# Causal attention with a two-layer local stack: side work placed one slot apart, one scratch buffer for the masked maxima, a second buffer for the outputs' second turn

## Chip, cores and metric

The kernel runs on one core of a Trainium2 chip. The metric is the device time of one execution in microseconds (us), the median of three runs.

## What is computed

An input x of 4 batches of 1024 tokens with 256 features goes through two residual blocks. The change touches only the first. Cut to that block:

```python
x = x + attn(layernorm(x))

def attn(x):                                   # B, T, D, H = 4, 1024, 256, 16 heads of 16
    q, k, v = heads(x @ wq + bq), heads(x @ wk + bk), heads(x @ wv + bv)
    scores = einsum('bhqd,bhkd->bhqk', q, k) / sqrt(16)
    p = softmax(scores + causal_mask, axis=-1)
    return merge(einsum('bhqk,bhkd->bhqd', p, v)) @ wo + bo

x = x + ffn_stack(layernorm(x))                # two layers of local attention (window 128) and gated FFN
```

All is float32. The second block starts from a layer norm of the first block's result; the first stage therefore hands over `y_sb`, that norm already taken, and a copy of x in device memory.

## The kernel before

The whole order of work is written out by hand (`tc.manual_schedule`): each engine executes its instructions in the order in which the program issues them. The first stage (the causal stage) ends at about 728 us of the trace, the rest is the local stack.

**Chunks and slots.** The causal stage goes through 16 chunks `n` (4 batches of 4 groups of 4 heads) in `NU` = 12 slots each, after a lead-in chunk `n` = -1. In slot `u` of chunk `n`, `pair(n, u, 0)` and `pair(n, u, 1)` issue on TensorE the transposed scores `t` of chunk `n` (for the exponentials) and the plain scores `s` of chunk `n + 1` (for the row maxima), two heads of each at a time (L417). ScalarE takes the exponential of `t` (L441), GpSimd zeroes what lies above the diagonal (L447, the select), and VectorE takes the maximum of `s`: with a plain reduction where no mask is needed (L435), else with an operation that adds the mask, writes the sum to a scratch tile `junk` that nothing reads, and leaves the maximum in `nmax` (L429). Each of these is followed by a short instruction that reads out the accumulator. Slots 0 to 3 and 8 to 11 have masked maxima of 512, 384, 256 and 128 columns (four each), slots 4 to 7 plain ones. The score tiles `s` have four banks of PSUM, shared with the projections; the tiles `t` have three. `products` (L480) multiplies the exponentials of two slots before (`LAG` = 2) with the values; its sum is copied to `avs` (L491).

**Side work.** At the end of slot `u`, the list `plan[n][u]` is issued. `put(n, u, fn, ...)` fills it; a slot number of 12 and more falls into the next chunk. The pieces are:

- `project`, `prep_b`: queries, keys and values of the next heads or the next batch, on TensorE with a copy on ScalarE; `prep_b` also has one GpSimd addition (L329).
- `norm(b, t0, t1)`: layer norm statistics of two tiles of x on VectorE (L263, L264, L158), then a power on GpSimd (L160). `prep_x`: the normalised tile `xn`, two on GpSimd (L274). `turn_x`: VectorE's 32 by 32 transposes of two tiles (L297), and on the second half of a group 16 DMAs on SP (L307) into `xnT`.
- `put_maxima`: a transpose of `nmax` on VectorE (L458) and five DMAs that put the maxima into the query tile.
- `put_out`: first turn of a finished output, `avs` to `t1`, on VectorE (L497), the reciprocal of the row sums (L499) and GpSimd's multiplication (L500). `put_oT`: second turn, `t1` to `t3`, on VectorE (L509), and four DMAs on SP into `oT` (L512).
- `out_b`: the output projection on TensorE (`pr`), a copy to `add` on ScalarE (L532) and the residual on GpSimd (L533); for the last two tile pairs of the last batch one addition by VectorE instead (L529). `out_s`: statistics on VectorE (L540, L541) and a power on GpSimd. `out_c`: `y_sb`, two GpSimd operations (L556).
- `spread`: DMAs that lay queries and keys out in strips; `scale_tab`: a multiplication of a table for the second block on GpSimd (L117), in chunk 5 only.

Three lists matter for the change: what the first chunk of a batch (c = 0) and the one behind it (c = 1) do for the next batch, the two turns of the outputs in every chunk, and what is left behind the last slot of chunk 15, which the schedule issues by hand. `a1`, `a2` and so on are pools of one, two and more buffers per tag; a tile of a tag takes the next of its buffers, and its first writer waits until the one who used that buffer last is done.

Of the kernel before, what the change touches and what calls it, by code (L numbers as in the profile page):

```python
# [10 lines left out]
F32 = mybir.dt.float32  # L11
# [5 lines left out]
P = 128  # L17
B, T, D = 4, 1024, 256
# [31 lines left out]
def kernel_body(  # L50
# [122 lines left out]
    with actx:  # L173
# [62 lines left out]
        NCH = B * NC4  # L236
# [96 lines left out]
        def bias():  # L333

            pb = one("pbias")
            for c in range(2):
                nc.tensor.transpose(
                    pb[:, c * P : (c + 1) * P], rows_c[:, 0, c * P : (c + 1) * P], ident
                )
            bv = a2.tile([P, 512], F32, tag="junk", name="bv")  # L340
            nc.scalar.copy(bv[:, 0:D], pb[:, 0:D])
            po = one("pbias_o")
            for c in range(2):
                nc.tensor.matmul(
                    po[:, 0:D], lhsT=bv[:, c * P : (c + 1) * P], rhs=wo_sb[:, c, :],
                    start=(c == 0), stop=(c == 1),
                )
            nc.vector.tensor_tensor(rows_c[:, 1, :], po[:, 0:D], rows_c[:, 1, :], ALU.add)
# [32 lines left out]
        def pair(n, u, pr):  # L381

            first, final = n < 0, n + 1 == NCH
            if (first or final) and pr:
                return
            th = () if first else range(4) if final else (2 * pr, 2 * pr + 1)
            sh = () if final else range(4) if first else (2 - 2 * pr, 3 - 2 * pr)  # L390

            def bank(pool, h):
                p, tag = ((pat, "t"), (pas, "s"))[pool]
                return p.tile([P, 512], F32, tag=tag, name=f"{'ts'[pool]}_{n}_{u}_{h}")

            todo = []
            if th:
                qb, kt = UNITS_T[u]
                c0 = max(0, kt * P - qb * 512)
                ts = {h: bank(final and h % 2, h) for h in th}  # L400
                for j, h in enumerate(th):
                    r = slice(32 * h, 32 * h + 32)
                    todo.append((j, 0, ts[h][:, c0:512], kTs(n)[r, kt * P : (kt + 1) * P],
                                 qTs(n)[r, qb * 512 + c0 : (qb + 1) * 512]))
            if sh:
                i, piece = UNITS_M[u]
                k0 = piece * 512
                k1 = min(k0 + 512, (i + 1) * P)
                w = k1 - k0
                diag = k1 == (i + 1) * P and piece == i // 4  # L410
                ss = {h: bank(not (first and h % 2), h) for h in sh}
                for j, h in enumerate(sh):
                    r = slice(32 * h, 32 * h + HD)
                    todo.append((j, 1, ss[h][:, 0:w], qTs(n + 1)[r, i * P : (i + 1) * P],
                                 kTs(n + 1)[r, k0:k1]))
            for j, _, o, lhsT, rhs in sorted(todo, key=lambda x: x[:2]):
                nc.tensor.matmul(o, lhsT=lhsT, rhs=rhs, start=True, stop=True)  # L417
            if sh:
                if i >= 4 and piece == 0 and pr == 0:
                    mxs[n + 1, i] = a5.tile([P, 4], F32, tag="mx", name=f"mx_{n + 1}_{i}")  # L420
                for h in sh:
                    first_of_two = i >= 4 and piece == 0
                    if first_of_two:
                        acc = mxs[n + 1, i][:, h : h + 1]
                    else:
                        acc = nmax[:, piece, 4 * h + i % 4 : 4 * h + i % 4 + 1]
                    if diag:
                        junk = a2.tile([P, 512], F32, tag="junk", name=f"junk_{n}_{u}_{h}")
                        nc.vector.tensor_tensor_reduce(  # L429
                            out=junk[:, 0:w], in0=ss[h][:, 0:w], in1=mask_c[:, 512 - w : 512],  # L430
                            scale=1.0, scalar=mxs[n + 1, i][:, h : h + 1] if piece else -3.0e38,
                            op0=ALU.add, op1=ALU.max, accum_out=acc,
                        )
                    else:
                        nc.vector.tensor_reduce(acc, ss[h][:, 0:w], AX.X, ALU.max)  # L435
                if piece and (pr or first):
                    del mxs[n + 1, i]
            for h in th:
                if h % 2 == 0:
                    et = a8.tile([P, 2, 512], F32, tag="et", name=f"et_{n}_{u}_{h}")  # L440
                nc.scalar.activation(et[:, h % 2, c0:512], ts[h][:, c0:512], AF.Exp, scale=ASCALE)  # L441
                if h % 2 == 0:
                    continue
                if kt >= 4 * qb:

                    d = et[:, :, c0 : c0 + P]
                    nc.gpsimd.affine_select(  # L447
                        out=d, in_=d, compare_op=ALU.is_ge, fill=0.0, base=0,
                        pattern=[[0, 2], [1, P]], channel_multiplier=-1,
                    )  # L450
                if h == 1:
                    avs_[n, u] = ([], c0)
                avs_[n, u][0].append(et)
# [51 lines left out]
        def put_oT(n, qb):  # L505

            b, c = divmod(n, NC4)
            t3 = a1.tile([P, 512], F32, tag="t3", name=f"t3_{n}_{qb}")
            nc.vector.transpose(t3, avs_.pop((n, "t1", qb)).rearrange("p q s -> p (q s)"))  # L509
            for j in range(4):  # L510
                r = (c % 2) * 64 + j * HD
                nc.sync.dma_start(  # L512
                    oT[r : r + HD, c // 2, qb * 512 : (qb + 1) * 512],
                    t3[STRIP * j : STRIP * j + HD, :],
                )

        def out_b(b, t2):

            pr = one(f"pr_{b}_{t2}")
            t0 = 2 * t2  # L520
            for i in range(2):
                for c in range(2):
                    strips(
                        pr[:, i * D : (i + 1) * D], oT[:, c, (t0 + i) * P : (t0 + i + 1) * P],
                        wo_sb[:, c, :], c,
                    )
            xt = xs[b][:, t0 : t0 + 2, :]
            if b == B - 1 and t2 >= 2:
                nc.vector.tensor_tensor(xt, pr.rearrange("p (i d) -> p i d", i=2), xt, ALU.add)  # L529
                return  # L530
            add = a1.tile([P, 2, D], F32, tag="add", name=f"add_{b}_{t2}")
            nc.scalar.copy(add, pr.rearrange("p (i d) -> p i d", i=2))  # L532
            nc.gpsimd.tensor_tensor(xt, xt, add, ALU.add)  # L533
# [31 lines left out]
        def put(n, u, fn, *a):  # L565

            plan[n + u // NU][u % NU].append((fn, a))

        def outs(n, u, b, t2):
            put(n, u, out_b, b, t2)  # L570
            put(n, u + 1, out_s, b, t2)
            put(n, u + 3, out_c, b, t2)

        def quarters(n, b, d, first, *slots):
            for i, u in enumerate(slots):
# [2 lines left out]
        for n in range(NCH):  # L578
            b, c = divmod(n, NC4)
            more = b + 1 < B  # L580
            if n >= 1:
                put(n, 2, put_out, n - 1, 1)
                put(n, 3, put_oT, n - 1, 1)
            if n + 1 < NCH:
                put(n, 4, put_maxima, n + 1, 0)
                put(n, 11, put_maxima, n + 1, 1)
            put(n, 6, put_out, n, 0)
            put(n, 7, put_oT, n, 0)
            if c == 0:
                if b:  # L590
                    quarters(n, b, 1, 3, 0, 2, 4, 6, 8)
                    outs(n, 7, b - 1, 2)
                    outs(n, NU, b - 1, 3)
                    put(n, 1, spread, n + 2, 0)
                    put(n, 3, spread, n + 3, 0)
# [4 lines left out]
                put(n, 9, spread, n + 2, 1)  # L600
                put(n, NU, spread, n + 3, 1)
            if c == 0 and more:
                for i, u in enumerate((5, 7, 9, 10)):
                    put(n, u, norm, b + 1, 2 * i, 2 * i + 2)
                put(n, 8, prep_x, b + 1, 0)
                put(n, 10, turn_x, b + 1, 0, 0)
                put(n, 10, prep_x, b + 1, 1)
                n += 1
                put(n, 0, turn_x, b + 1, 0, 1)
                put(n, 1, prep_x, b + 1, 2)  # L610
                put(n, 2, prep_x, b + 1, 3)
                put(n, 3, turn_x, b + 1, 1, 0)
                put(n, 4, turn_x, b + 1, 1, 1)
                quarters(n, b + 1, 0, 0, 5, 6, 8, 10)
                n += 1
                quarters(n, b + 1, 0, 4, 0, 2, 3, 4)
# [6 lines left out]
                quarters(n, b + 1, 1, 0, 3, 5, 7)  # L623
                n -= 3
            if c == 3:
                outs(n, 9, b, 0)
                outs(n, 11, b, 1)
        n = -1
        plan[n][0] = [(project, (0, 0, i, 3)) for i in range(2)]
        plan[n][0] += [(spread, (0, 1, nc.scalar)), (spread, (1, 0)), (spread, (1, 1))]  # L630
# [19 lines left out]
        with tc.manual_schedule(  # L650
# [42 lines left out]
            for w in range(LAG, 0, -1):  # L693
                products(NCH - 1, NU - w)
            left = [x for u in plan[NCH] for x in u]
            for fn, a in left[0:1]:
                fn(*a)
            put_out(NCH - 1, 1)
            for fn, a in left[1:]:
                fn(*a)  # L700
            put_oT(NCH - 1, 1)
            for fn in (out_b, out_s, out_c):
                for t2 in (2, 3):
                    fn(B - 1, t2)
# [646 lines left out]
```

## Time and profile before

| what | value |
|---|---|
| median of 3 runs | 1962.36 us (1960.04 to 1964.89) |
| the profiled execution, its own time | 1962.94 us |
| its span in the trace | 1960.9 us |
| granted TensorE clock over the span | 0.97 |
| TensorE, matmul busy | 1888.3 us (96%) |
| VectorE busy | 1350.1 us (69%) |
| ScalarE busy | 1005.1 us (51%) |
| GpSimd busy | 1031.2 us (53%) |
| causal stage, lead-in and preparation included | to about 728 us |
| last output's DMA of the causal stage | 724.7 to about 728.6 us |

How to read it: all times of the trace are microseconds from the span's start. PE is TensorE's matmuls, PEld its weight loads, DVE is VectorE, ACT is ScalarE, POOL is GpSimd, SP is SyncE, which here issues nearly all DMAs. L429 is line 429 of the kernel. A timeline's line has start, duration, engine, line, operation, output and inputs, shape and count, and in brackets the idle time of the engine before it with what ended it. In a table of windows each line has the busy time and the number of instructions of each engine, and after them the clock that TensorE was granted (1.00 is full speed, 0.50 half). Matmuls of this stage use a quarter of TensorE's rows or columns, and in the trace up to four of them overlap, so that the busy share stays near full even when only one of the four runs.

### The profile page before, as it was taken

How to read it: one execution, taken by the hardware profiler on the slowest of the kernel's cores; microseconds unless marked ns; L12 is line 12 of the kernel's file. 1: busy time of each engine (PE TensorE's matmuls, PEld its weight loads, DVE VectorE, ACT ScalarE, POOL GpSimd, SP SyncE). 2: the span in 40 equal slices, each digit the busy share in tenths (PEclk: the TensorE clock that was granted, in tenths of full speed). 3: DMA queues.
4: the chain of work that ended last, by engine and by line, in shares of the span. 5: the costliest groups of instructions: out<-in, count | busy, mean ns of one | idle time of the engine just before them, and what ended most of it. 6: DMA issues, size and time to landing. Idle time of an engine off the chain costs nothing.

```text
span 1960.9 us, 51320 instructions
## 1 busy us (share of the span) xinstructions
PE 1888.3 (96%) x19234; PEld 1031.0 (53%) x19234; DVE 1350.1 (69%) x4092; ACT 1005.1 (51%) x2646; POOL 1031.2 (53%) x1268
## 2 busy tenths in 40 slices
PE   8999999999999978899899999999999999999999
PEld 5333333333333335556566665666566566566575
DVE  6766776677677825666776787687677677677633
ACT  1546545564565654454455545545554554554521
POOL 3322362245234138675775676676675676676621
PEclk8979989998999988999999999999999999999999
DMA  4122111212201001155555555555565655665520
GB/s 119 22 34 75 26 33 32 61 24 36 62 12 28 10 32 67 27 93 90 93 97 99 88 103 99 117 106 103 102 143 100 105 110 104 116 109 95 101 49 22
DMA packets 797927, 144.43 MB, mean 74 GB/s; under 512 B 766336, under 2 KB 788592, under 8 KB 797168
## 3 DMA queue, kind: packets, MB, share of 16 engines
q1 hardware_dynamic: 797424, 140.89, 37.1%
q8 instruction: 153, 2.51, 0.5%
q14 instruction: 94, 0.77, 0.1%
q10 hardware_dynamic: 256, 0.26, 0.1%
HBM read 21.25 MB, written 8.65 MB: 15 GB/s over the span
## 4 chain that ended last, share of the span: by engine, by line
PE 86%; SPq 4%; DVE 3%; issue 2%; POOL 2%; ACT 1%; DMA 1%; DVEq 0%; POOLq 0%; ACTq 0%
PE t L417 15%; PE pag L1151 15%; PE pf L1175 8%; PE av L480 7%; PE pw L1061 6%; PE pq L792 5%; PE pk L792 5%; PE pv L792 5%; PE plo L1019 4%; PE ls L939 4%; SPq L891 3%; PE pp L251 3%; PE pv L251 2%; PE s L417 2%; PE pr L251 2%
## 5 line engine op out<-in xcount | busy, mean ns | idle before, releaser
L441 ACT ACTIVATE et<-t 128x512 f32<-128x512 f32 (+2 forms) x744 | 327.7, 490 | 232.5 <-PE s L417 210.9
L417 PE MATMUL t<-qbuf,kbuf 32*128 32x512 f32 (+2 forms) x1488 | 396.3, 552 | 2.5 <-ACT et L441 2.4
L417 PE MATMUL s<-kbuf,qbuf 16*128 16x512 f32 (+3 forms) x1440 | 382.1, 554 | 1.5 <-DVE mx L435 1.1
L1151 PE MATMUL pag<-hnT,w 128*128 128x512 f32 x704 | 312.5, 593 | 0.8 <-DVE hnT L1135 0.8
L972 ACT ACTIVATE e<-e,lnmx 128x192 f32<-128x192 f32 (+2 forms) x512 | 224.1, 439 | 48.7 <-DVE lnmx L965 48.2
L417 PEld LDWEIGHTS t<-qbuf,kbuf 32*128 32x128 f32 x1488 | 143.9, 189 | 168.9 <-ACT et L441 111.5
L447 POOL TENSOR_SCALAR_AFFINE_SELECT et<-et 128x256 f32<-128x256 f32 x256 | 103.0, 410 | 221.4 <-ACT et L441 221.1
L986 POOL TENSOR_SCALAR e<-e,lrsum 128x192 f32<-128x192 f32 (+2 forms) x512 | 206.7, 430 | 20.1 <-DVE lrsum L983 14.7
L1151 PEld LDWEIGHTS pag<-hnT,w 128*128 128x128 f32 x704 | 131.9, 191 | 143.1 <-issue 134.9
L480 PE MATMUL av<-et,v_sb 128*32 128x256 f32 (+5 forms) x2240 | 186.8, 405 | 6.5 <-POOL et L447 4.7
L435 DVE TENSOR_REDUCE mx<-s 128x1 f32<-128x512 f32 x240 | 153.1, 681 | 57.2 <-PE s L417 55.0
L831 POOL TENSOR_TENSOR rn<-ss,mhalf 128x16 f32<-128x16 f32 x64 | 188.1, 2940 | 5.3
L1175 PE MATMUL pf<-w,act 128*128 128x256 f32 x768 | 173.1, 379 | 0.0
L828 POOL TENSOR_TENSOR rot<-rot,m 128x1024 f32<-128x1024 f32 x64 | 151.3, 2365 | 35.4 <-DVE m L809 29.7
L1175 PEld LDWEIGHTS pf<-w,act 128*128 128x128 f32 x768 | 145.8, 190 | 26.6 <-issue 7.2
L1165 DVE SCALAR_TENSOR_TENSOR act<-pag,cols_sb,ge 128x512 f32<-128x512 f32 x80 | 59.3, 741 | 142.3 <-ACT ge L1164 98.7
L429 DVE CUSTOM_DVE_ANT_0 junk<-s,mask_c 128x512 f32<-128x512 f32 (+3 forms) x240 | 106.7, 484 | 62.4 <-PE s L417 59.6
L417 PEld LDWEIGHTS s<-kbuf,qbuf 16*128 16x128 f32 x1440 | 141.8, 189 | 10.8 <-DVE mx L435 4.6
L429 DVE CUSTOM_DVE_ANT_0 junk<-s,mask_c,mx 128x512 f32<-128x512 f32 (+3 forms) x240 | 120.9, 546 | 37.6 <-PE s L417 36.4
L965 DVE CUSTOM_DVE_ANT_0 e<-ls,mask_h 128x192 f32<-128x192 f32 x408 | 116.9, 350 | 23.6 <-PE ls L939 23.6
L480 PEld LDWEIGHTS av<-et,v_sb 128*32 128x32 f32 x2240 | 45.4, 109 | 164.1 <-issue 116.0
L1061 PE MATMUL pw<-wlo,loT 128*128 128x256 f32 x512 | 128.6, 394 | 0.8 <-ACT loT L1052 0.7
(294 smaller groups left out, 3372.4 us busy)
## 6 DMA issues: line engine op xcount, KB each, us to landing
ring_sb<-turned SPq DMA_DIRECT2D x896, 96.0 KB
qbuf<-dense SPq DMA_DIRECT2D x128, 32.0 KB
oT<-t SPq DMA_DIRECT2D x128, 32.0 KB
x_keep<-x SPq DMA_DIRECT2D x4, 1024.0 KB
xr<-x_keep SPq DMA_DIRECT2D x8, 512.0 KB
out_dram<-y_sb SPq DMA_DIRECT2D x16, 256.0 KB
kbuf<-dense SPq DMA_DIRECT2D x120, 32.0 KB
x<-in_x_dram SPq DMA_DIRECT2D x3, 1024.0 KB
```

The source lines that it names most:

```text
L417: nc.tensor.matmul(o, lhsT=lhsT, rhs=rhs, start=True, stop=True)
L429: nc.vector.tensor_tensor_reduce(out=junk[:, 0:w], in0=ss[h][:, 0:w], in1=mask_c[:, 512 - w : 512], scale=1.0, scalar=mxs[n + 1, i][:, h : ...
L435: nc.vector.tensor_reduce(acc, ss[h][:, 0:w], AX.X, ALU.max)
L441: nc.scalar.activation(et[:, h % 2, c0:512], ts[h][:, c0:512], AF.Exp, scale=ASCALE)
L480: nc.tensor.matmul(av[32 * j : 32 * j + 32, lo:hi], lhsT=v_sb[b % 2][:, kt, VW * (4 * c + j) : VW * (4 * c + j) + STRIP], rhs=ets[j // 2][ ...
L792: nc.tensor.matmul(pq[i], lhsT=lhs[c], rhs=wt[:, c, i * INNER : (i + 1) * INNER], start=(c == 0), stop=(c == 1),)
L831: nc.gpsimd.tensor_tensor(rn[:, :, 0], ss, mhalf, ALU.pow)
L972: nc.scalar.activation(e[:, i, lo:nk], e[:, i, lo:nk], AF.Exp, bias=nmx[:, h : h + 1], scale=-1.0, accum_out=sums[:, h : h + 1],)
L986: nc.gpsimd.tensor_scalar(e[:, i, lo:nk], e[:, i, lo:nk], rsum[:, h : h + 1], 1.0, ALU.mult, ALU.mult)
L1061: nc.tensor.matmul(pw[:, 0:D], lhsT=oT[:, c, :], rhs=wt[:, c, :], start=(c == 0), stop=(c == 3))
L1151: nc.tensor.matmul(pg[half], lhsT=wt[:, c, ff * P : (ff + 1) * P], rhs=hnT[:, c, :], start=(c == 0), stop=(c == 1),)
L1175: nc.tensor.matmul(pf[:, 0:D], lhsT=act[:, f, i * P : (i + 1) * P], rhs=wt[:, f, :], start=(f == 0), stop=(f == NF - 1),)
```

## The change

- The scratch tile `junk` has one buffer instead of two. The tile `bv` of `bias` moves to the tag `add`.
- `put_oT` comes two slots after `put_out` instead of one (slots 4 and 8 instead of 3 and 7), and its tile `t3` has two buffers instead of one.
- In chunks with c = 0, the four `norm`s move from slots 5, 7, 9, 10 to 0, 1, 3, 5; the four `prep_x` from 8, 10, 13, 14 to 7, 9, 12, 14; the four halves of `turn_x` from 10, 12, 15, 16 to 10, 11, 15, 17.
- `out_b`, `out_s`, `out_c` of the first tile pair move from slots 9, 10, 12 to 10, 11, 13 of the last chunk of a batch; for the second and third pair `out_s` and `out_c` come one slot later.
- All residuals of the last batch are added by VectorE.
- Behind the last slot, `put_out` and `put_oT` of the last output come ahead of the rest.

```diff
-            bv = a2.tile([P, 512], F32, tag="junk", name="bv")
+            bv = a1.tile([P, 512], F32, tag="add", name="bv")
...
-                        junk = a2.tile([P, 512], F32, tag="junk", name=f"junk_{n}_{u}_{h}")
+                        junk = a1.tile([P, 512], F32, tag="junk", name=f"junk_{n}_{u}_{h}")
...
-            t3 = a1.tile([P, 512], F32, tag="t3", name=f"t3_{n}_{qb}")
+            t3 = a2.tile([P, 512], F32, tag="t3", name=f"t3_{n}_{qb}")
...
-            if b == B - 1 and t2 >= 2:
+            if b == B - 1:
...
-        def outs(n, u, b, t2):
+        def outs(n, u, b, t2, wait=1):
             put(n, u, out_b, b, t2)
-            put(n, u + 1, out_s, b, t2)
-            put(n, u + 3, out_c, b, t2)
+            put(n, u + wait, out_s, b, t2)
+            put(n, u + wait + 2, out_c, b, t2)
...
-                put(n, 3, put_oT, n - 1, 1)
+                put(n, 4, put_oT, n - 1, 1)
...
-            put(n, 7, put_oT, n, 0)
+            put(n, 8, put_oT, n, 0)
...
-                    outs(n, 7, b - 1, 2)
+                    outs(n, 7, b - 1, 2, 2)
...
-                for i, u in enumerate((5, 7, 9, 10)):
+                for i, u in enumerate((0, 1, 3, 5)):
                     put(n, u, norm, b + 1, 2 * i, 2 * i + 2)
-                put(n, 8, prep_x, b + 1, 0)
+                put(n, 7, prep_x, b + 1, 0)
+                put(n, 9, prep_x, b + 1, 1)
                 put(n, 10, turn_x, b + 1, 0, 0)
-                put(n, 10, prep_x, b + 1, 1)
+                put(n, 11, turn_x, b + 1, 0, 1)
                 n += 1
-                put(n, 0, turn_x, b + 1, 0, 1)
-                put(n, 1, prep_x, b + 1, 2)
+                put(n, 0, prep_x, b + 1, 2)
                 put(n, 2, prep_x, b + 1, 3)
                 put(n, 3, turn_x, b + 1, 1, 0)
-                put(n, 4, turn_x, b + 1, 1, 1)
+                put(n, 5, turn_x, b + 1, 1, 1)
...
-                outs(n, 9, b, 0)
-                outs(n, 11, b, 1)
+                outs(n, 10, b, 0)
+                outs(n, 11, b, 1, 2)
...
-            for fn, a in left[0:1]:
+            put_out(NCH - 1, 1)
+            put_oT(NCH - 1, 1)
+            for fn, a in left:
                 fn(*a)
-            put_out(NCH - 1, 1)
-            for fn, a in left[1:]:
-                fn(*a)
-            put_oT(NCH - 1, 1)
```

## Prediction

> Terms: chunk c0 to c15 is one round of twelve slots in the causal stage (batch times four plus head group), s0 to s11 its slots; the lead-in before c0 has scores only.
>
> **What bounds the kernel now.** I read the page first, then the busy time and granted clock of one window per chunk, then windows of 3.4 us around the places where the clock fell, then the timelines there. Busy shares say little: PE is at 96% everywhere. The table by chunk says more (columns: window, length, busy us and count of PE, PEld, DVE, ACT, POOL, then PE's clock, DMA share, GB/s).
>
> ```profile
> 92.60:142.40 49.80, 49.58 (x416) 17.35 (x412) 32.57 (x105) 23.75 (x55) 15.83 (x26) 0.73 0.20 33
> 268.40:320.30 51.90, 48.66 (x436) 17.00 (x432) 33.34 (x110) 24.50 (x56) 26.24 (x34) 0.84 0.19 32
> 446.40:494.90 48.50, 47.14 (x438) 16.88 (x434) 33.24 (x110) 24.52 (x56) 21.69 (x32) 0.86 0.20 35
> 619.70:656.70 37.00, 36.45 (x399) 14.24 (x395) 29.85 (x96) 22.48 (x52) 13.62 (x25) 1.00 0.08 17
> 656.70:692.10 35.40, 34.85 (x376) 13.51 (x372) 28.73 (x91) 21.86 (x51) 7.67 (x18) 1.00 0.12 40
> ```
>
> c1, c5 and c9 take 49.8, 51.9 and 48.5 us, c13 (same place in its batch, no next batch to prepare) 37.0. Four projections of about 1 us each (two take 1.93 in the chain of waits) explain 4.2; so c5 loses 10.7, c9 7.3, and c1, which has no 1.9 us output projection, 10.5. Their clock is 0.73 to 0.86. The windows around c5's start show how:
>
> ```profile
> 263.40:266.80 3.40, 3.36 (x39) 1.58 (x37) 3.29 (x14) 1.70 (x7) 3.40 (x6) 1.00 0.10 23
> 266.80:270.20 3.40, 3.28 (x33) 1.60 (x34) 3.30 (x18) 1.29 (x4) 3.40 (x5) 1.00 0.00 0
> 270.20:273.60 3.40, 3.40 (x18) 0.72 (x17) 1.72 (x7) 0.61 (x2) 3.40 (x5) 0.50 0.02 2
> ```
>
> DVE (3.3 of 3.4) and POOL (3.4) are full for 6.8 us, PE starves for score banks, and the clock is halved from 270.2 to 277.0. The same happens at 96.1 (27.3 us long, until c1's first projections) and at 447.7 (6.8 us). Two more falls, at 290.6 and 468.1, follow a wait for POOL. The timelines show the two kinds of wait:
>
> ```profile
> 93.83 0.18 PEld L417 LDWEIGHTS s<-kbuf,qbuf 16*128 16x128 f32 x1 [0.95 <-DVE nmax L429]
> ...
> 463.33 0.77 DVE L297 STREAM_TRANSPOSE xturn<-xn 128x256 f32<-128x256 f32 x2
> 466.96 0.71 DVE L509 STREAM_TRANSPOSE t<-t 128x512 f32<-128x512 f32 x1 [2.86 <-POOL t L500]
> ```
>
> So the stage is PE-bound, with VectorE's lateness deciding where the clock falls.
>
> **The change, part by part.** Durations are this profile's; its span is 1960.9 and its own time 1962.9, 2.0 around it and 0.6 above the median.
>
> *Second turn of outputs two slots on.* At 466.96 DVE stood 2.86 us behind L500 on POOL. In c9 the multiply would be done some 9.9 us into s1, and DVE reaches the turn in s4 at about 10.6: the wait goes, and with it the fall at 468.1 (c9's s5 lasts 8.7 us, c13's 3.2, a projection 1.0: 4.5 too long). In c5 the fall at 290.6 has another cause, POOL's table scaling (2.36 us twice); it stays, and the queue is now add 1.28, two xn 2.45, scale 2.36 in s0, so the selects of s1 and s2 come some 2.7 us late instead of 2.16: gain 0, from -1 to +2.
>
> *Spread of norm, prep_x, turn_x.* A norm costs DVE 1.45 (264.24 to 265.69), an out_s 1.27, a turn_x 0.68, the two turns of outputs 0.9 and 0.6. Before, s9, s10 of c4 held norm, norm and turn_x. After, s9 to s11 hold out_s, turn_x, turn_x; for c0 only the two turns. Second halves of turn_x issue 16 DMAs on SP at 0.6 us each (four take 2.4) one slot sooner; ahead of them is the maxima's copy, behind them only copies used a chunk later: 0. But s1 of c4 and c8 now holds out_s and norm together: 2.72 us of DVE.
>
> *One scratch buffer for the masked maxima.* This is the new wait. Masked maxima follow one another without a pause today:
>
> ```profile
> 648.97 0.75 DVE L429 CUSTOM_DVE_ANT_0 junk<-s,mask_c,mx 128x512 f32<-128x512 f32 x1 [0.28 <-PE s L417]
> 649.65 0.08 DVE L429 DVE_READ_ACCUMULATOR2_ANT nmax<- 128x1 f32 x1
> 649.65 0.75 DVE L429 CUSTOM_DVE_ANT_0 junk<-s,mask_c,mx 128x512 f32<-128x512 f32 x1
> ```
>
> Start to start is 0.68, less than one lasts. The view of L429 has this beside its 512 maxima:
>
> ```profile
> L429 DVEq EVENT_SEMAPHORE  x386: 21/21/50, 22.8 to 691.8; - x193
> ```
>
> These are the sequencer's waits for the scratch buffer; in the trace one ends 0.03 us after the accumulator read of the maximum before last, when nothing is lost. With one buffer it must be the last one. What such a wait costs when it binds is seen once:
>
> ```profile
> 736.60 0.42 DVE L540 BATCH_NORM_STATS2 sto<-x 128x6 f32<-128x256 f32 x1
> 737.12 0.18 DVE L541 BATCH_NORM_AGGREGATE mvo<-sto 128x2 f32<-128x6 f32 x1
> ```
>
> 0.10 from end to start behind a sequencer wait. So start to start becomes 0.75 + 0.10 = 0.85: +0.18 (bounds: 0, if PE always keeps DVE waiting, and 0.19). The Trainium skill speaks against this: VectorE: DVE Perf Modes, The DRAIN you can't avoid, measured eight copies with a semaphore after each at the same time as with one after the last, so the semaphore would be free. By that rule this edit costs 0; by the rows, where neighbours overlap by 0.07, 0.18 each. I take the rows. 480 such maxima in c0 to c14 are 86 us of DVE, nearly all beside PE work: a clean slot's DVE work rises from 2.4 to 3.0 us in s0 (slot 3.28), 1.9 to 2.6 in s1 (2.64), 1.1 to 1.8 in s11 (1.79). In c14 DVE still fits into 35.4 (about 33): loss 0.3 at s11. Nothing is left for side work in s1, s2, s10, s11.
>
> *Where it comes through.* Rule used: DVE's lag at the next slot is its lag now, plus its work, minus the slot's length; PE stalls by lag plus first pair of maxima minus slot length. (It gives 0.9 and 1.5 for c4's s10 and s11 before; seen: 0.9 and about 1.3.) After, in c4 and c8: s0 4.4 of work against 3.87, s1 5.2 against 2.64, s2 2.8 against 3.61: the lag reaches 4.3, and PE stalls 0.36, 1.3 and 0.8. At s10, s11: 0.7 and 0.8. In c0, s10 and s11: 0.4.
>
> *Price of a stall.* The Trainium skill, TensorE: Matmul & The Clock Gate, What's actually happening, wants about one idle window (3.4 us) before the clock halves; by it these stalls cost themselves only. The rows show halving after windows with some 1.3 us of starving, and none after stalls of 0.3 to 0.9. I take the rows: 3.4 us more (6.8 at half clock) for a window that loses over 1.1 us.
>
> *Residual by VectorE, last batch.* Two more batches of ACT 0.59 and POOL 1.27 go, two DVE adds of 0.69 come in c15, where DVE is idle: about -1 on ACT, which sets c15. *Tail order.* The multiply waited for the y_sb pair:
>
> ```profile
> 720.90 2.44 POOL L556 TENSOR_SCALAR y_sb<-x,mvo,rs_o 128x256 f32<-128x256 f32 x2
> 723.30 0.62 POOL L500 TENSOR_TENSOR t<-t,rec 128x256 f32<-128x256 f32 x1
> ```
>
> rec ends at 721.4, so -1.9. y_sb's pairs now end near 726.7, before the last projections' adds: hidden. Second t3 buffer and bv's place: 0.
>
> **Sum.** Gains: c1's fall -9.5; c5's and c9's start, where stalls of 1.5 remain and the fall is even odds, -1.9 each; c9's second fall -4.5; tail -3: 20.8. Losses: lead-in, where DVE runs 22.1 to 29.2 and 45.4 to 53.5 without a pause, 30 waits of 0.18 less what PE hides: 4, with a stall and half a fall in c0, 2.5; c4 and c8 2.4 stall and four fifths of a fall each: 10.4; out_s in c5, c9, c13 0.8 each, last chunks 1: 3.4. Together 20.3. Net -0.5 against 1962.9: about 1962.4.
>
> **Rivals.** (1) *The scratch wait does not bind* (PE's banks release the maxima anyway, or the rule holds). Then c4's s1 leaves a stall of 0.4 to 0.7 only, no fall; c1 -10, c5 and c9 -5 each, c9 -4.5, tail -3, second fall of c5 stays: -27, 1936; half of the wait gives some 1950. For it: 139 of the maxima wait for PE's scores (96 us). Against it: at the loaded slots DVE is full. 26%. (2) *Slower: the clock, once halved in c4 and c8, stays down* as at 96.1, where 27.3 us cost 10.5 because no projection came. Two such instead of 2.7 each: +15.6, 1978. It decides once s1 to s3 lose over 1.1 us in one window. Against it: c4 and c8 have projections in s2, s4 and s6, and the falls with projections near lasted 6.8 and 10.2 us. Half of it, with all 30 waits of the lead-in bare (5.4 instead of 4), gives 1971. 36%, other ways to be slower included. (3) *The spreading does not do what it says*: c5's POOL queue, above, at most +2, inside the others. Likeliest, 38%: gains given back, 1962.
>
> **Numbers.** Within 0.3% is 5.9 us, what a measurement can tell. Faster 0.26, same 0.38, slower 0.36. Likeliest case alone: 1956 to 1968. The range takes in half of each rival: 1946 to 1979.
>
> **What would show it.** Masked maxima 0.85 apart instead of 0.68 where DVE is behind, 0.80 without the mx operand. c1 near 40 us at clock 1.00. c4 and c8 longer than 40.9 and 40.6, clock under 1.00 near their s3. The 2.86 us wait at L509 gone. Oddly placed falls, or maxima still 0.68 apart, would prove the sum wrong.

## The result and the profile after

The changed kernel takes 1972.7 us (median of 18 runs, 1964 to 1982 but for one of 2007) against 1962.4 us for the kernel before, run beside it on the same chip: a ratio of 1.005, with a 95% interval of 1.0037 to 1.0064. So it is slower by half a per cent, where 1962 and no difference were forecast. The profiled execution took 1976.7 us with a span of 1975.0; before it was 1962.9 and 1960.9. The span grew by 14.0 us, and all of it can be found chunk by chunk. This execution is 4.0 us above its kernel's median, the one of before 0.6 above: so some 3 of the 14 us may belong to the execution and not to the change.

The table of windows of the changed kernel has the same columns as the one of before (window, length, busy us and count of PE, PEld, DVE, ACT, POOL, PE's clock, DMA share, GB/s). The lines are the lead-in, c1, c4, c5, c8, c9 and c14.

```profile
21.50:62.70 41.20, 38.12 (x300) 15.52 (x296) 26.18 (x76) 4.86 (x13) 4.95 (x4) 0.71 0.25 71
103.40:143.30 39.90, 38.98 (x413) 15.18 (x409) 32.34 (x97) 23.54 (x54) 12.22 (x22) 1.00 0.23 39
229.80:279.20 49.40, 47.26 (x455) 17.14 (x451) 37.35 (x119) 25.39 (x57) 23.68 (x33) 0.85 0.10 22
279.20:331.00 51.80, 49.92 (x437) 17.54 (x433) 35.08 (x100) 24.07 (x55) 24.06 (x32) 0.75 0.19 33
416.10:468.00 51.90, 49.77 (x452) 17.59 (x448) 37.13 (x117) 25.39 (x57) 22.96 (x32) 0.80 0.09 21
468.00:508.40 40.40, 40.06 (x436) 15.65 (x432) 33.47 (x104) 23.94 (x55) 20.10 (x32) 1.00 0.23 39
676.40:713.10 36.70, 36.15 (x375) 15.02 (x371) 29.95 (x90) 21.77 (x50) 7.71 (x19) 1.00 0.11 36
```

Read it by the clock column. c1 and c9 are now at full clock and 40 us long, as intended: 9.9 and 8.1 us won. c4 and c8, which took 40.9 and 40.6 before, are at 0.85 and 0.80 and take 49.4 and 51.9. c5 fell before and falls still. The lead-in went from 32.1 to 41.1. c14 has no fall at all and still is 1.2 longer, as it is 1.0 longer with the one scratch buffer alone (experiment 2) and not at all with two (experiment 1).

The cause of that can be seen on VectorE's timeline, in c14 as before (start, duration, engine, line, operation):

```profile
667.85 0.75 DVE L429 CUSTOM_DVE_ANT_0 junk<-s,mask_c,mx 128x512 f32<-128x512 f32 x1 [0.20 <-PE s L417]
668.52 0.08 DVE L429 DVE_READ_ACCUMULATOR2_ANT nmax<- 128x1 f32 x1
668.75 0.75 DVE L429 CUSTOM_DVE_ANT_0 junk<-s,mask_c,mx 128x512 f32<-128x512 f32 x1
669.43 0.08 DVE L429 DVE_READ_ACCUMULATOR2_ANT nmax<- 128x1 f32 x1
```

The read of the accumulator ends at 668.60, the next maximum starts at 668.75: 0.15 of nothing, and start to start is 0.90 where it was 0.68. Without the `mx` operand it is 0.85 (65.23 to 66.08) where it was 0.61. No bracket stands behind the 0.15, as no other engine is named for it: VectorE waits for its own last operation. The gap is 0.14 to 0.15 at all widths of masked maxima in this profile. The view of L429 shows the sequencer's waits, 454 in place of 386:

```profile
L429 DVEq EVENT_SEMAPHORE  x454: 21/21/21, 23.5 to 713.7; - x152
```

The table of waits says who is late now (total us, times, longest):

```profile
DVE junk L429 <- PE s L417: 47.6, 70, 2.9
...
PEld pp L251 <- DVE nmax L429: 20.2, 27, 2.4
```

VectorE waits half as long for scores as before (96.0 us in 139 waits), and the projections wait longer for a masked maximum (11.6 in 16 before, none over 0.8). Where this takes the clock down is seen in windows of 3.4 us around s2 of c4:

```profile
235.40:238.80 3.40, 3.40 (x38) 1.23 (x33) 2.93 (x12) 2.01 (x6) 3.21 (x5) 1.00 0.26 59
238.80:242.20 3.40, 1.42 (x20) 0.59 (x16) 2.86 (x14) 0.66 (x2) 2.84 (x5) 0.70 0.23 53
242.20:245.60 3.40, 3.40 (x40) 1.44 (x32) 2.21 (x10) 1.21 (x5) 1.03 (x2) 0.50 0.20 43
245.60:249.00 3.40, 3.40 (x25) 0.72 (x17) 2.57 (x9) 1.03 (x3) 3.11 (x4) 0.50 0.00 0
```

TensorE works 1.42 of 3.4 us, and from 240.2 on the clock is 0.50, for 13.7 us (in c8 for 20.5, from 427.9). The timeline of that place shows what stood in TensorE's way:

```profile
237.99 0.42 DVE L540 BATCH_NORM_STATS2 sto<-x 128x6 f32<-128x256 f32 x1
...
239.26 0.42 DVE L263 BATCH_NORM_STATS2 st<-x 128x6 f32<-128x256 f32 x1
...
240.47 0.17 DVE L158 TENSOR_SCALAR ve_a<-mv 128x2 f32<-128x2 f32 x1
240.54 0.42 DVE L429 CUSTOM_DVE_ANT_0 junk<-s,mask_c 128x256 f32<-128x256 f32 x1
...
240.89 0.08 DVE L429 DVE_READ_ACCUMULATOR2_ANT nmax<- 128x1 f32 x1
...
241.02 0.65 PE L251 MATMUL pp<-xnT,wq_sb 128*32 128x256 f32 x4 [1.99 <-DVE nmax L429]
```

`out_s` (from 237.99) and `norm` (from 239.26) stand together in s1 and take VectorE till 240.54. Only then does the first maximum of s2 run; it frees a score bank, and the projection of s2, which takes one of the same four banks, has waited 1.99 us for it.

The 2.86 us of VectorE behind GpSimd's multiply are gone; all that is left of waits at L509 is 2.8 us in three, from 10.9 in eight:

```profile
  POOL t L500: 2.8, 3
```

At the end of the stage the multiply now comes ahead of the `y_sb` pair, and the output projection's wait for its DMA fell from 8.46 us to 6.70. The lines are of GpSimd's and then of TensorE's timeline:

```profile
742.35 0.62 POOL L500 TENSOR_TENSOR t<-t,rec 128x256 f32<-128x256 f32 x1 [2.46 <-DVE rec L499]
742.96 2.43 POOL L556 TENSOR_SCALAR y_sb<-x,mvo,rs_o 128x256 f32<-128x256 f32 x2
```

```profile
747.65 0.66 PE L251 MATMUL pr<-wo_sb,oT 128*32 128x256 f32 x4 [6.70 <-DMA oT<-t]
```

The forecast's sum beside the two profiles (us, after minus before; chunk lengths from TensorE's first score matmul of a chunk to that of the next; the forecast's `out_s` losses are put into their chunks):

| where | forecast | profiles |
|---|---|---|
| lead-in and c0 | +6.5 | +10.3 |
| c1 | -9.5 | -9.9 |
| c4 and c8 | +10.4 | +19.8 |
| c5 | -1.1 | -0.1 |
| c9 | -5.6 | -8.1 |
| c10 to c14 | +1.8 | +7.5 |
| c15 and behind it | -3.0 | -6.9 |
| c3 and c7; start | 0 | +0.9; +0.6 |
| sum | -0.5 | +14.0 |

### The profile page after: what moved, and what is told of

Its sections match the earlier page's. It is cut to its first block, busy times and chain, and to the rows that moved or that the text cites. A ratio compares the mean times of both kernels' runs of the same rounds, so it can differ in the third digit from the quotient of the medians.

```text
span 1975.0 us, 51398 instructions
## 1 busy us (share of the span) xinstructions
PE 1902.0 (96%) x19234; PEld 1038.3 (53%) x19234; DVE 1376.9 (70%) x4094; ACT 1002.6 (51%) x2644; POOL 1027.4 (52%) x1266
## 4 chain that ended last, share of the span: by engine, by line
PE 87%; DVE 4%; SPq 4%; issue 2%; DMA 1%; POOL 1%; ACT 1%; DVEq 0%; POOLq 0%; ACTq 0%
PE t L417 16%; PE pag L1149 15%; PE pf L1173 8%; PE av L480 8%; PE pw L1059 6%; PE pq L790 5%; PE pk L790 5%; PE pv L790 5%; PE plo L1017 4%; PE ls L937 4%; SPq L889 3%; PE pp L251 3%; PE s L417 2%; PE pr L251 2%; PE pv L251 2%
## 5 line engine op out<-in xcount | busy, mean ns | idle before, releaser
L417 PE MATMUL s<-kbuf,qbuf 16*128 16x512 f32 (+3 forms) x1440 | 391.8, 556 | 2.2 <-DVE nmax L429 1.6
L417 PE MATMUL t<-qbuf,kbuf 32*128 32x512 f32 (+2 forms) x1488 | 391.7, 555 | 1.5 <-ACT et L441 1.5
L429 DVE CUSTOM_DVE_ANT_0 junk<-s,mask_c,mx 128x512 f32<-128x512 f32 (+3 forms) x240 | 131.6, 548 | 52.5 <-PE s L417 26.0
L417 PEld LDWEIGHTS s<-kbuf,qbuf 16*128 16x128 f32 x1440 | 147.4, 191 | 9.1 <-DVE nmax L429 5.1
L429 DVE CUSTOM_DVE_ANT_0 junk<-s,mask_c 128x512 f32<-128x512 f32 (+3 forms) x240 | 116.8, 487 | 48.1 <-PE s L417 21.6
```

Of the source, the lines that this page charges most:

```text
L429: nc.vector.tensor_tensor_reduce(out=junk[:, 0:w], in0=ss[h][:, 0:w], in1=mask_c[:, 512 - w : 512], scale=1.0, scalar=mxs[n + 1, i][:, h : ...
```

## The experiments

**Theory S**: the wait for the one scratch buffer carries the loss; the new places of the side work are good or harmless without it. **Rival P**: the new places carry the loss (`out_s` and `norm` together in s1), and the scratch wait is only VectorE time that TensorE hides. Ratios below are against the kernel before, run beside the experiment; intervals are 95%.

**1. The change with two scratch buffers.** For want of room `t3` goes back to one buffer; all else is the changed kernel.

```diff
-                        junk = a1.tile([P, 512], F32, tag="junk", ...)
+                        junk = a2.tile([P, 512], F32, tag="junk", ...)
...
-            t3 = a2.tile([P, 512], F32, tag="t3", ...)
+            t3 = a1.tile([P, 512], F32, tag="t3", ...)
```

> The changed kernel with two scratch buffers for the masked maxima again, and one buffer for the second turn's tile; all else of the change stays. Theory S (the wait for the single scratch buffer carries the loss): masked maxima again 0.61 to 0.68 us apart (512 columns), lead-in back from 41 to about 32 us, chunks 4 and 8 back from 49.4 and 52.0 to about 40, chunks 1 and 9 stay near 40: 1936 to 1946 us. Rival P (the new places of the side work carry it, above all statistics of outputs and of the next batch in slot 1 of chunks 4 and 8, and the wait is free): within 5 us of the changed kernel, 1966 to 1976.

Measured: 1934.1 us, ratio 0.9869 (0.9839 to 0.9899). S holds, and by far: everything of the change but the scratch and `t3`'s second buffer is worth 26 us, and the total lies just below the range expected. The lead-in took 35.0 us in this profile, not the 32 expected; experiment 5, with the same lead-in, took 32.2 (see "Open" below). Its windows of c1, c4, c5, c8 and c9:

```profile
94.20:134.00 39.80, 37.88 (x416) 14.58 (x412) 30.72 (x97) 23.50 (x55) 12.50 (x23) 1.00 0.23 40
218.90:259.90 41.00, 39.55 (x452) 14.66 (x448) 35.05 (x117) 25.06 (x57) 22.27 (x31) 1.00 0.11 23
259.90:309.30 49.40, 47.95 (x436) 16.60 (x432) 32.15 (x104) 24.18 (x57) 25.32 (x34) 0.79 0.22 38
394.20:435.10 40.90, 39.45 (x452) 14.62 (x448) 34.93 (x116) 25.06 (x57) 22.30 (x31) 1.00 0.11 25
435.10:474.70 39.60, 39.05 (x440) 14.95 (x436) 32.12 (x104) 24.13 (x57) 20.71 (x32) 1.00 0.23 40
```

c4 and c8 are back at full clock with `out_s` and `norm` together in s1 still: the projection of c4's s2 waits there too, but its weight load stands 1.59 us and not 2.39, and the clock holds. The one fall left between the lead-in and 678 us is in c5.

**2. The kernel before with one scratch buffer** (and `bv` in the tag `add`), nothing else.

```diff
-            bv = a2.tile([P, 512], F32, tag="junk", name="bv")
+            bv = a1.tile([P, 512], F32, tag="add", name="bv")
...
-                        junk = a2.tile([P, 512], F32, tag="junk", ...)
+                        junk = a1.tile([P, 512], F32, tag="junk", ...)
```

> The kernel before with one scratch buffer for the masked maxima and nothing else (the bias row's tile moved to another tag, to have its place). Theory S: masked maxima 0.84 instead of 0.61 us apart where VectorE is behind, lead-in 41 us, all falls of the clock in chunks 1, 5 and 9 stay: 1975 to 1990 us. Rival P: same as before, 1960 to 1965.

Measured: 1985.0 us, ratio 1.012 (1.0084 to 1.0155): +23 us by the scratch alone (`bv` has its new place in experiment 1 too and does no harm there). Its lead-in and its c1:

```profile
20.80:61.80 41.00, 37.92 (x298) 15.36 (x294) 26.12 (x75) 4.86 (x13) 4.95 (x4) 0.71 0.25 72
102.90:156.70 53.80, 53.70 (x412) 18.50 (x408) 33.89 (x103) 23.56 (x54) 15.83 (x26) 0.65 0.18 31
```

The lead-in is 41.0 as in the changed kernel (41.1), against 32.1: so these 9 us are the scratch's and not the norms'. c4 and c8 take 43.5 and 43.2 us, 2.6 more than before, and have no long fall. c10 to c14 take 4.5 us more, without a fall. The fall of c1 lasts 37.5 us here instead of 27.3.

**3. The change with the norms apart**: one scratch buffer stays, but no `norm` is in s1 with `out_s`.

```diff
-                for i, u in enumerate((0, 1, 3, 5)):
+                for i, u in enumerate((0, 3, 5, 7)):
```

> The changed kernel, still with one scratch buffer, but with the four norms in slots 0, 3, 5 and 7 instead of 0, 1, 3 and 5, so that slot 1 of chunks 4 and 8 has the outputs' statistics alone. Theory S: lead-in stays 41 us, chunks 4 and 8 lose some of their stall in slots 2 to 4 but not all: 1958 to 1968. Rival P: all of chunks 4 and 8's loss goes, 1950 to 1956.

Measured: 1962.1 us, ratio 1.0004 (0.9983 to 1.0024), 10.6 us below the changed kernel's median. The lead-in, c4 and c8:

```profile
20.80:61.70 40.90, 37.82 (x298) 15.28 (x294) 26.11 (x75) 4.86 (x13) 4.95 (x4) 0.71 0.25 72
228.00:270.80 42.80, 41.94 (x455) 16.23 (x451) 36.65 (x118) 25.34 (x57) 23.43 (x33) 0.99 0.11 25
407.90:450.30 42.40, 41.53 (x452) 16.20 (x448) 36.63 (x117) 25.34 (x57) 22.94 (x32) 1.00 0.12 26
```

The falls of c4 and c8 are gone, the lead-in is not touched. The total is within S's range. So rival P has a true part: c4 and c8 fall only where both come together, the scratch wait and the two pieces in s1; taking either away cures them (experiments 1 and 3). S has the greater part: the lead-in answers to the scratch only, the last chunks mostly. c12 to c14 take 112.0 us before and 112.1 in experiment 1, 116.2 with the scratch alone (experiment 2), and 120.2 here, of which a fall of 6.8 us in c13 is some 3.4.

**4. The kernel before with the second turn two slots on**, and with the first pair's output in slot 10.

```diff
-                put(n, 3, put_oT, n - 1, 1)
+                put(n, 4, put_oT, n - 1, 1)
...
-            put(n, 7, put_oT, n, 0)
+            put(n, 8, put_oT, n, 0)
...
-                outs(n, 9, b, 0)
+                outs(n, 10, b, 0)
```

> The kernel before with the outputs' second turn two slots behind the first (slots 4 and 8) and the first output projection of a batch one slot later; nothing else of the change. Theory S and the prediction alike: VectorE's wait of 2.86 us for GpSimd's multiplication in chunk 9 goes, and with it the clock's fall at 468, -4.5; the falls at 96, 270, 290 and 448 stay: 1955 to 1960 us. Rival P expects no gain: 1960 to 1965.

Measured: 1958.3 us, ratio 0.9989 (0.997 to 1.0008). In time this decides nothing: some 2 us won with an interval that includes none. In the profile the fall of c9's second part lasts 3.4 us (from 463.5) instead of 6.8, so the forecast's 4.5 us for it were too much where the fall at c9's start stays: the window 438.5 to 485.4 is still at 0.89. The other falls did not all stay, as had been expected: c1's lasts 6.8 us here and not 27.3 (in experiment 10, where c1 is as before, it is 10.2 and 3.4), and c5 has one fall of 6.8 instead of two (45.8 us long). These runs don't show what of c5's gain is the edit's.

```profile
438.50:485.40 46.90, 44.57 (x436) 16.26 (x432) 33.17 (x110) 24.19 (x56) 21.62 (x32) 0.89 0.22 37
```

**5. Experiment 1 with GpSimd's table scaling elsewhere.** The two multiplications of 2.36 us stood in c5's s0 and s1, behind the residual's and the `xn` operations.

```diff
-        put(5, 0, scale_tab, 0, 0)
-        put(5, 1, scale_tab, 0, 1)
+        put(6, 4, scale_tab, 0, 0)
+        put(6, 5, scale_tab, 0, 1)
```

> The changed kernel with two scratch buffers (one for the second turn's tile), and the two table scalings of GpSimd moved from slots 0 and 1 of chunk 5 to slots 4 and 5 of chunk 6, where GpSimd has no select to do. Theory: what is left of falls, the 20.5 us at half clock in chunk 5, comes from GpSimd's queue (the select of slot 1 behind add, two xn and a scaling): chunk 5 from 49.4 to about 41, 1924 to 1929 us. Rival: the add and the xn alone make the selects late enough, or VectorE is behind it: 1931 to 1936.

Measured: 1927.1 us, ratio 0.9836 (0.9821 to 0.9852). c5 takes 39.9 at full clock:

```profile
258.70:298.60 39.90, 38.93 (x436) 14.91 (x432) 31.94 (x104) 23.97 (x56) 20.66 (x32) 1.00 0.24 42
```

After the lead-in's no fall is left until 694 us. That the scaling is what holds c5 back, as the forecast said, is borne out for this kernel.

**6. Experiment 5 with the norms apart** (slots 0, 3, 5, 7, as in experiment 3).

> As the run with the table scalings moved, and the norms in slots 0, 3, 5, 7: takes VectorE's 1.2 us lateness for the projection in slot 2 of chunks 4 and 8 away. Theory of the lag (late maxima hold the bank that a projection needs): another -2 to -3, 1921 to 1926 us. Rival (1.2 us in a slot of 3.6 are made up later): same as the run beside it.

Measured: 1925.0 us, ratio 0.9819 (0.9799 to 0.984). c4 and c8 come down to 39.7 and 39.8 from 41.0; in the profiled run c5 has one fall of 3.4 us (43.8 long, against 49.4 in experiment 1, whose clock raster lies alike). The intervals of experiments 5 and 6 overlap: no difference that these runs can tell.

**7. The kernel before with the table scaling elsewhere**, the edit of experiment 5 alone.

> The kernel before with the two table scalings moved to slots 4 and 5 of chunk 6 and nothing else. If GpSimd's queue of scalings alone makes the fall at 290 in chunk 5: chunk 5 from 51.9 to 45, 1953 to 1957 us. If the second turn that waits for GpSimd would make it fall anyway, as in chunk 9: 48.5 like chunk 9, 1958 to 1961.

Measured: 1961.0 us, ratio 0.9997 (0.9979 to 1.0015): the expectation missed, its rival was right. With the scaling gone from c5 the second turn still waits there for GpSimd's multiply, as in c9 before, and the clock falls at 291.3 instead of 290.6:

```profile
289.80 0.71 DVE L509 STREAM_TRANSPOSE t<-t 128x512 f32<-128x512 f32 x1 [2.87 <-POOL t L500]
```

In the kernel before, the same turn stood even longer in c5. The trace puts its wait down to a DMA, but the multiply, behind a table scaling, had ended only 0.03 us sooner:

```profile
291.34 0.63 POOL L500 TENSOR_TENSOR t<-t,rec 128x256 f32<-128x256 f32 x1
...
292.00 0.71 DVE L509 STREAM_TRANSPOSE t<-t 128x512 f32<-128x512 f32 x1 [5.59 <-DMA xnT<-xturn]
```

So the scaling was one part of a queue that made the turn late, and taking it away alone is not enough.

**8. The change with the masked scores written over the scores themselves**, in PSUM. No scratch at all; `t3` keeps its two buffers.

```diff
-                        junk = a1.tile([P, 512], F32, tag="junk", ...)
...
-                            out=junk[:, 0:w], in0=ss[h][:, 0:w], ...
+                            out=ss[h][:, 0:w], in0=ss[h][:, 0:w], ...
```

> The changed kernel, but the masked maxima write their sum over the scores in PSUM that they read, so that there is no scratch tile and no wait between neighbours; the second turn keeps its two buffers. Theory S: maxima 0.61 to 0.68 us apart as with two scratch buffers, 1930 to 1940 us. If the price came from anything else that the change does to these instructions, or if writing to PSUM is slower than to SBUF by over 0.1 us each: 1955 to 1975.

Measured: 1928.9 us, ratio 0.9865 (0.9825 to 0.9904). VectorE's timeline (L428 is the maximum here):

```profile
59.50 0.60 DVE L428 CUSTOM_DVE_ANT_0 s<-s,mask_c 128x384 f32<-128x384 f32 x1
60.02 0.14 DVE L428 DVE_READ_ACCUMULATOR2_ANT nmax<- 128x1 f32 x1
60.02 0.60 DVE L428 CUSTOM_DVE_ANT_0 s<-s,mask_c 128x384 f32<-128x384 f32 x1
```

Here maxima follow one another 0.52 apart (384 columns; 0.48 with two scratch buffers, 0.71 with one); over the whole profile the commonest distance is 0.48, and 0.62 for 512 columns, as with two. The time is just below the range expected. The line has 70 sequencer waits instead of 454, as each score tile is another place, and neither the buffer for `t3` nor the scratch has to be given up. c5 stays at full clock in this profile with the table scaling still in it, though it takes 42.1: so the scaling makes the fall likely, and doesn't make it certain.

**9. Experiment 8 with the table scaling elsewhere and the norms apart.**

> The changed kernel with the masked maxima written over their scores, the table scaling in c6 (slots 4 and 5) and the norms in slots 0, 3, 5 and 7. Theory (the scratch wait, the late selects of c5 and the norm in s1 are all that hold the causal stage back): c4 and c8 near 39.8, c5 near 40, no fall of the clock between 40 and 690 us; 1924 to 1929, as with two scratch buffers. Rival: writing to PSUM (384 columns 0.60 us instead of 0.55, the read of the accumulator 0.14 instead of 0.08) leaves VectorE less room, some slot falls again: 1930 to 1936.

Measured: 1928.9 us, ratio 0.9827 (0.9804 to 0.9851). c4, c5 and c8 take 40.1 each at full clock, and no fall is left between 48 and 668 us; one of 3.4 us comes at 668.8, where none was expected. It can't be told from experiments 5, 6 and 8.

**10. The kernel before with only the two edits at the end.**

```diff
-            if b == B - 1 and t2 >= 2:
+            if b == B - 1:
...
-            for fn, a in left[0:1]:
-                fn(*a)
             put_out(NCH - 1, 1)
-            for fn, a in left[1:]:
-                fn(*a)
             put_oT(NCH - 1, 1)
+            for fn, a in left:
+                fn(*a)
```

> The kernel before with only the two edits at the end: all residuals of the last batch by VectorE, and the last output's turns ahead of what is left over. The prediction booked 3 us for them (1.9 of order, 1 of ScalarE in c15). If the whole is right: ratio 0.9985, 1958 to 1960 us, the last chunk 23.3. If ScalarE gives nothing in c15, as the profile of the changed kernel suggests: last chunk 24.3, its wait for the last output's DMA 1.8 shorter, ratio 0.999, which this measurement can hardly tell from none; the profile decides.

Measured: 1958.1 us, ratio 0.9981 (0.9969 to 0.9993), 3.7 us won. c15 takes 24.3 as before, so ScalarE's freed microsecond gives nothing. On GpSimd the multiply leads, and on TensorE the projection waits 6.72 us where it was 8.46:

```profile
719.54 0.62 POOL L500 TENSOR_TENSOR t<-t,rec 128x256 f32<-128x256 f32 x1 [3.17 <-DVE rec L499]
720.15 2.43 POOL L556 TENSOR_SCALAR y_sb<-x,mvo,rs_o 128x256 f32<-128x256 f32 x2
```

```profile
724.85 1.51 PE L251 MATMUL pr<-wo_sb,oT 128*32 128x256 f32 x12 [6.72 <-DMA oT<-t]
```

From c15's last score matmul to the end of the span it is 1237.7 us, against 1244.5 before. Over all profiles the eight kernels with the new tail lie at 1236.0 to 1237.7, the four with the old one at 1240.8 to 1245.2. The wait explains 1.7 of it. Behind it the clock stood at half for 38.7 us in all in this profile and for 48.9 in that of before, and half of that difference is the other 5. Why a start sooner by 1.7 us shortens those stretches wasn't tried.

## Why the prediction was wrong

**Right in kind.** The forecast put the new wait where it is, on the masked maxima, against the rule that a semaphore costs nothing; it named c4 and c8 as the places of new falls, the lead-in as a loss, c1 and c9 as gains, c5's queue on GpSimd as untouched, c9's wait at L509 as gone. Experiments 1, 2 and 8 confirm the wait as the cause of the loss: taken out of the change, put into the kernel before, and taken out another way. The first rival priced the change without that wait at 1936, and experiment 1 measured 1934.

**The step that failed** is the price of the scratch wait, in two terms of the sum. Of the 14.5 us between forecast and profile, c4 and c8 have 9.4, c10 to c14 5.7, lead-in and c0 3.8; the tail and c9 give 6.4 back. The time itself lies in the wide range given, 1946 to 1979; what failed is the sum in its middle.

- *The gap.* "0.10 from end to start behind a sequencer wait. So start to start becomes 0.75 + 0.10 = 0.85: +0.18". It is 0.90, +0.22, and +0.24 without `mx`. The 0.10 came from one pair of other operations on the same engine; between a maximum's accumulator read and the next maximum it is 0.15. One pair was taken for the price, and the upper bound given, 0.19, left no room for another pair to be dearer. A quarter to a third more on each of some thirty bare waits in the lead-in and on four per slot in c10 to c14 is small alone; but VectorE's masked slots had been reckoned as just full, so what was added had no cover. For c14 the forecast's "about 33" of 35.4 us was short even by its own price: 28.7 and 32 times 0.18 is 34.5. So c10 to c14 lost 7.5 us where 1.8 were booked, some 1.7 of it by a fall of 3.4 us in c13. With the scratch alone they lost 4.5 without a fall (experiment 2).
- *What a late slot costs.* "PE stalls by lag plus first pair of maxima minus slot length": stalls of 0.36, 1.3 and 0.8 were booked in c4's s1 to s3. The rule counted the score matmuls alone. The projection in s2 takes one of the same four banks, and it stood for 1.99 us in one piece. Still the stalls were not booked too low in all: of the 8.5 and 11.3 us that c4 and c8 lost, half of the falls' length is 6.9 and 10.3, which leaves 1.6 and 1.0 for stalls, where 2.5 each had been booked. The length of the falls is what failed. It was booked by a rule, "3.4 us more (6.8 at half clock) for a window that loses over 1.1 us", that the runs don't bear out: in the prediction's own line from 266.80 TensorE loses 0.12 us and the clock falls, and in experiment 6 a step that lost 1.63 us had no fall behind it (last section). And "the falls with projections near lasted 6.8 and 10.2" was the argument against the second rival: here projections are what stalled, and the falls lasted 13.7 and 20.5. Thus 19.8 in place of 10.4. In the lead-in the same: half clock for 13.7 and 10.2 us (10.2 before), +9.0 where 4 were booked.

So the second rival is what happened, in its milder form: half of the long falls with all waits of the lead-in bare gave 1971, and 1972.7 was measured. That it is so near is luck in part: the last chunks cost 5.7 us more than booked, the tail and c9 gave 6.4 more. The rival held 36% with the other slow cases against 38% for the sum that came out even. The even sum was the difference of 20.8 gained and 20.3 lost, and the losses were counted with the shortest falls of this part of the trace, while the gains stood in it as measured.

**Smaller terms.** c1: right (-9.5, -9.9). c9: -8.1 for -5.6, because no fall came at its start, where even odds had been given; the fall behind the turn alone is worth less than the 4.5 booked (experiment 4). c5: right that it stays, and experiment 5 bears out the cause where the second turn is out of the way; in the kernel before that turn stood in c5 too, 5.59 us behind the scaling and still 2.87 without it (experiment 7). The tail: -3 was less than half of what the profiles show (-6.9), and for another reason than ScalarE in c15, which gave nothing.

**Open.** How long a fall lasts differs from execution to execution of the same instructions. Experiment 10 changes nothing ahead of c15, yet in its profile the lead-in takes 34.9 us and c1 46.0, against 32.1 and 49.8 before. Within a profile the clock changes only on a raster of 3.41 us, and where the raster lies goes with the result: in the four profiles without the scratch wait whose lead-in took 32.1 to 32.6 us, a step begins 0.0 to 0.5 us behind the lead-in's first score matmul, in the five with 34.9 to 35.3 us it begins 2.5 to 3.1 us behind it. In the three with one buffer (41.0 and 41.1 us) it begins from 0.2 ahead to 0.2 behind, so compared like with like the scratch costs the lead-in 8 to 9 us. What such a place loses is thus known from a single profile only to some 3 or 4 us. Nothing here moved the raster on purpose, and why c5 fell in experiment 6 and not in 5 or 9 is not known.

## What to carry to other kernels

A scratch output that nobody reads still orders its writers: with one buffer each operation waits until the one before has read out its accumulator, and here that cost 0.22 to 0.24 us on operations of 0.3 to 0.75. Before giving such a tile one buffer to make room, write the result over the operand instead, if nothing reads that again; it needs no tile at all. And when side work is moved in a kernel near the limit of its clock, add up each slot for every engine, count everything that takes a bank of the shared pool and not the main matmuls alone, and price a stall by the half clock that may follow it, which here cost more than the stall itself.

## What the runs showed of the hardware that was not expected

- A wait of VectorE for its own last operation: 0.15 us from the end of the accumulator read to the next start, against an overlap of 0.07 us where nothing is waited for.
- Half clock held for 13.7 us in c4 (from 240.2) and 20.5 in c8, though TensorE was shown busy nearly all through; 37.5 us was the longest (experiment 2). How long TensorE stood still does not tell when the clock falls: in experiment 1 a step of the raster with 1.2 us lost (2.19 busy of 3.40) was followed by a fall, in experiment 6 one with 1.6 lost was not:

```profile
268.90:272.30 3.40, 2.19 (x28) 1.14 (x20) 3.01 (x16) 1.12 (x5) 3.40 (x4) 1.00 0.28 44
272.30:275.70 3.40, 3.40 (x28) 1.42 (x28) 1.19 (x6) 0.45 (x2) 3.40 (x5) 0.50 0.35 52
```

```profile
111.89:115.30 3.41, 1.78 (x24) 0.81 (x24) 1.20 (x3) 0.37 (x1) 0.00 (x0) 1.00 0.29 55
115.30:118.70 3.40, 3.40 (x32) 1.17 (x32) 2.20 (x4) 2.35 (x5) 0.00 (x0) 1.00 0.24 56
```

- What goes with it is the work done in a step. Take every matmul record's streamed columns times the share of a 128 by 128 array that it fills (an eighth for `16*128`, a quarter for `32*128` or `128*32`; one that crosses the end of a step counts by its part), and add these up over a step of the raster. In the causal stages of the twelve profiles the next step is at half clock if this sum is under 1500, at full clock if it is over: 2322 of 2334 steps fall in with that, 11 of the other 12 have between 1469 and 1531, and it holds at full clock and at half alike. The two steps above have 1283 and 1567. Of the eight at half clock in c1 before, the first seven have 1052 to 1515 and the last, which ended the fall, 1633. So the score matmuls, with few rows, can hold the clock down while TensorE looks busy. This was found in the traces afterwards; no run tested it.
- Writing 384 masked columns to PSUM took 0.60 us and not 0.55 behind another maximum, and the accumulator's read behind it 0.14 and not 0.08. The overlap hides this in most places: the commonest distance from start to start is 0.48, as with two scratch buffers.
